# Gating guidance steps by their inputs' expected times, opening the last image with one chunk, and taking an image's last statistics from PSUM

## The chip, the cores and the metric

The kernel runs on one core of a Trainium2 chip. The metric is device time in microseconds, from the first to the last instruction of one execution. The kernel before takes 3024.74 us (median of 3 runs, 3021.86 to 3026.59); the profiled execution spans 3024.8 us. A difference of about 0.2% is the least that can be told from none.

## What is computed

The input x is (4, 256, 48, 48). Layer 0 adds to x an attention block: group norm, a 3x3 convolution with batch norm and ReLU, an 8-head attention over all 2304 pixels, a projection. Layer 1 adds to that a block of dynamic filters, and this is where the change lies:

```python
def _dyn_branch(x, w, d):                 # one dilation
    xp = jnp.pad(x, ((0, 0), (0, 0), (d, d), (d, d)))
    out, k = jnp.zeros_like(x), 0
    for dy in (-d, 0, d):
        for dx in (-d, 0, d):
            patch = xp[:, :, d + dy:d + dy + H, d + dx:d + dx + W]
            out = out + patch * w[:, k:k + 1]
            k += 1
    return out

guidance = _conv(x, W_cat, pad=1)         # 256 -> 45 channels, 3x3
outs = [x]
for i, d in enumerate((1, 6, 12, 24, 36)):
    w = jax.nn.softmax(guidance[:, 9 * i:9 * (i + 1)], axis=1)
    outs.append(_dyn_branch(x, w, d))
y = _conv(jnp.concatenate(outs, axis=1), W_scale, pad=0)   # 6*256 -> 256, 1x1
# then y is normalised over the whole batch: mean and variance of each channel
```

Here x is the group norm of the layer's input, and the layer's input is added to the result. So each pixel has 45 weights of its own, nine for each of five dilations, softmaxed over the nine.

## The kernel before

**Layout.** 256 channels are two halves (NH = 2) of 128 partitions. An image's 2304 pixels are six chunks (NCK = 6) of eight rows, CH = 384 pixels. The schedule is manual: each engine runs its instructions in the order in which the Python program emits them.

**Stages.** For each image: convolution and q, k, v (conv_qkv), attention, then dynamic_filters. The filters of image b are interleaved with conv_qkv of image b+1, a generator called `other`, of which every step is one matmul (or a small group) on PE and what follows from it. The filters of the last image (b = 3, `alone` in the code) have no other work beside them. Behind them comes finish, the batch norm over the whole batch and the output.

**Filters of one image.** A generator, weights(c), makes the softmaxed weights ("guidance") for two chunks c and c+1: 36 tap matmuls (18 for each chunk, which sit side by side in PE's columns, chunk c in PSUM partitions 0 to 44 and chunk c+1 in 64 to 108 of the tile pg; L1106), two copies to SBUF, one on ACT (L1116) and one on DVE (L1117), three transposes (tile pt, L1124), maximum, subtraction, exponential on ACT, sum, reciprocal and two products on DVE (L1137 to L1154), and for each of the two chunks three transposes back (tile pw, L1162), a rounding copy on ACT (L1169) and a subtraction of the rounded part on DVE (L1170), which gives the tile w. pg, pt and pw share one PSUM buffer (misc). In the profile a matmul of this kernel's 4-byte data shows as two records.

Then for each chunk, dilation and tap: PE spreads row k of w over all partitions by a matmul with pick (tile wb, L1299; three PSUM buffers, five when alone), DVE multiplies it with the shifted image (the first tap into cat, L1322; the others into prod, L1332, five buffers), and POOL adds prod to cat (L1349). When a cat is complete, PE mixes it with W_scale into py (L1240). In the last image some products skip POOL and are mixed straight from prod (`single`), where the program's clocks see POOL far behind PE. When a chunk is mixed, ACT copies py to SBUF (L1259), DVE takes the batch norm's statistics from the copy (L1263), and a DMA stores it.

**What sets the order.** The program keeps a model clock for each engine: clock(engine, ns, *after) starts an instruction behind the engine's last one and 150 ns behind each time in `after`. Before it emits a wb, it calls fill(until), where `until` is the expected time at which the wb buffer comes free. As long as PE's model clock is behind that time, fill emits, in this order of preference: a mix from `queue` whose input is expected by now, a guidance step if the pace allows one (pace[0] grows with the taps emitted, 27.6 steps in two chunks; pace[1] counts the steps taken), a step of `other`. Guidance of pair c+2 is paced over chunks c and c+1 and finished off, whatever is left, at the end of chunk c+1. The guidance of chunks 0 and 1 comes before the first tap ("opening"), with steps of `other` put in for as many ns as its negative yields say.

```python
def fill(until):
    while clock.t["PE"] < until:
        if queue and when(queue[0]) <= clock.t["PE"]:
            queue.pop(0)[-1]()
            continue
        if pace[1] < pace[0] and next(ahead, None) is not None:
            pace[1] += 1
            continue
        if next(other, None) is None:
            return
```

## Time and profile before

| stretch (us from the start) | what | length |
|---|---|---|
| 532 to 867, 1255 to 1594, 1981 to 2317 | filters of images 0, 1, 2 beside the next image's convolution | 335, 339, 336 |
| of these 571 to 853, 1294 to 1580, 2019 to 2303 | their taps | 282, 286, 284 |
| 2701 to 2737 | last image: projection, norm, opening | 36 |
| 2737 to 2981 | last image: taps | 244 |
| 2981 to 3017 | last mixes, batch norm, output | 36 |

The rest is the first convolution and four attentions, which the change doesn't touch. Over the span PE is busy 2834.9 us (94%), DVE 2419.1 (80%), ACT 1549.8 (51%) and POOL 1109.4 (37%). The granted clock of PE is 0.978 of full speed in the mean; in the filter stages it falls to one half for stretches of 3.4 to 10.2 us.

How to read a line of the timeline: start, time from the first start to the last end of the merged instructions, engine, source line, operation, output tile <- input tiles, shape, number of instructions; in brackets the idle time of the engine just before, and who released it. A line of the stage table has the stretch, its length and then busy us (and instructions) of PE, PEld, DVE, ACT and POOL, the clock granted to PE, the mean share of the DMA engines and GB/s. A busy share alone doesn't tell a bound: PE and POOL are both near 90% in the taps, so the places where one of them rests, and what the other does then, have to be laid side by side.

### The profile page before, as it was taken

To read this page: it belongs to the slowest core of one execution; us is meant where nothing else is said; L and a number is where in the kernel's file an instruction comes from. 1 tells how busy PE (TensorE), PEld (TensorE's weight loads), DVE (VectorE), ACT (ScalarE), POOL (GpSimd) and SP (SyncE) were. 2 spreads that over 40 slices of the span, in tenths; PEclk is the share of its full clock that TensorE was granted. 3 is DMA by queue.
4 is the path that set the end of the run, shared out by engine and by line. 5 is a ranking of instruction groups with operands and counts; after the bars stand their busy time and mean duration, and the time that the engine had idled before them with its cause. 6 is when DMAs were issued, how large, how long until landed. Compare 5 with 4: busy or idle time off the path is not lost. (4 is left out here: it accounts for less than half of the span.)

```text
span 3024.8 us, 42936 instructions
## 1 busy us (share of the span) xinstructions
PE 2834.9 (94%) x17454; PEld 1303.8 (43%) x17454; DVE 2419.1 (80%) x2312; ACT 1549.8 (51%) x1812; POOL 1109.4 (37%) x842
## 2 busy tenths in 40 slices
PE   7999999998999999989899999998899999989894
PEld 5622224465542222556662222346555222245552
DVE  6399999678869999767868999966776999976676
ACT  3489878201158888600228987830114888760003
POOL 1000000898930000389880000078894000007884
PEclk9999999999999999999999999999999999999997
DMA  4400000011030000001003000000002000012004
GB/s 173 97 1 6 7 11 7 27 37 32 22 79 6 3 4 12 22 25 36 29 11 79 6 6 12 6 27 27 21 6 42 3 5 6 12 66 112 1 1 178
DMA packets 77965, 95.52 MB, mean 32 GB/s; under 512 B 52144, under 2 KB 66752, under 8 KB 75968
## 3 DMA queue, kind: packets, MB, share of 16 engines
q1 hardware_dynamic: 76960, 87.31, 10.1%
q0 software_dynamic: 800, 5.41, 0.5%
q8 instruction: 138, 2.26, 0.3%
q14 instruction: 67, 0.55, 0.1%
HBM read 62.03 MB, written 30.67 MB: 31 GB/s over the span
## 5 line engine op out<-in xcount | busy, mean ns | idle before, releaser
L945 ACT ACTIVATE p<-se 128x1024 f32<-128x1024 f32 x1296 | 1259.0, 1026 | 243.0 <-PE se L936 217.2
L983 DVE TENSOR_TENSOR acc<-acc,p 128x2048 f32<-128x2048 f32 x536 | 1227.9, 2291 | 71.2 <-ACT p L945 24.3
L1349 POOL TENSOR_TENSOR cat<-cat,prod 128x752 f32<-128x752 f32 (+7 forms) x743 | 994.9, 1349 | 549.1 <-DVE prod L1332 507.5
L936 PE MATMUL se<-q,k 32*128 32x512 f32 (+1 forms) x5760 | 802.9, 591 | 6.0 <-DVE pad L1050 2.5
L1332 DVE TENSOR_TENSOR prod<-wb,pad 128x768 f32<-128x768 f32 (+7 forms) x768 | 553.5, 748 | 226.6 <-POOL cat L1349 151.0
L966 PE MATMUL num<-p,vT 128*32 128x512 f32 (+1 forms) x5760 | 692.9, 561 | 8.6 <-ACT scratch L988 7.4
L936 PEld LDWEIGHTS se<-q,k 32*128 32x128 f32 x5760 | 292.4, 183 | 519.7 <-issue 309.4
L738 POOL TENSOR_TENSOR cv_q<-pad,cv_q 128x600 f32<-128x600 f32 x3 | 4.1, 1353 | 1322.5 <-ACT cv_q L736 1322.5
L1299 PE MATMUL wb<-w,pick 128*128 128x384 f32 (+3 forms) x888 | 395.5, 495 | 11.7 <-DVE prod L1332 10.0
L1240 PE MATMUL py<-cat,wsc 128*128 128x384 f32 x960 | 354.9, 497 | 5.5 <-POOL cat L1349 5.3
L966 PEld LDWEIGHTS num<-p,vT 128*32 128x32 f32 x5760 | 121.7, 108 | 485.2 <-issue 437.5
L1299 PEld LDWEIGHTS wb<-w,pick 128*128 128x128 f32 x888 | 168.4, 194 | 151.9 <-DVE prod L1332 57.1
L1240 PEld LDWEIGHTS py<-cat,wsc 128*128 128x128 f32 x960 | 180.3, 193 | 92.4 <-POOL cat L1349 9.7
L844 PE MATMUL pc<-cv_q,u 128*128 128x288 f32 x576 | 170.2, 429 | 12.1 <-DVE cv_q L740 7.0
L844 PE MATMUL pc<-cv_k,u 128*128 128x288 f32 x576 | 161.1, 411 | 9.5 <-DVE yt L784 7.2
L1106 PE MATMUL pg<-pad,wcat 128*45 128x384 f32 x864 | 151.5, 494 | 1.5 <-DVE pad L590 1.5
L874 PE MATMUL pq<-hid,wqkv 128*128 128x384 f32 x384 | 136.1, 487 | 6.0 <-DVE yt L784 6.0
L844 PEld LDWEIGHTS pc<-cv_q,u 128*128 128x128 f32 x576 | 113.1, 201 | 41.9 <-DVE cv_q L740 7.0
L766 ACT ACTIVATE hid<-yt,bn_t_f,bn_s 128x288 f32<-128x288 f32 x64 | 39.4, 626 | 174.2 <-DVE yt L779 103.0
L844 PEld LDWEIGHTS pc<-cv_k,u 128*128 128x128 f32 x576 | 107.5, 191 | 38.6 <-DVE yt L784 8.4
L1322 DVE TENSOR_TENSOR cat<-wb,pad 128x768 f32<-128x768 f32 x120 | 113.9, 949 | 3.5 <-PE wb L1299 3.0
L983 DVE TENSOR_TENSOR acc<-p,p 128x2048 f32<-128x2048 f32 x36 | 82.5, 2292 | 40.3 <-ACT p L945 40.3
(209 smaller groups left out, 1613.5 us busy)
## 6 DMA issues: line engine op xcount, KB each, us to landing
pad<-in_x SPq DMA_DIRECT2D x14, 1152.0 KB, 14.9
u<-u_d SPq DMA_DIRECT2D x18, 768.0 KB, 4.3
x_d<-pad SPq DMA_DIRECT2D x48, 192.0 KB, 2.5
xst<-in_x SPq DMA_DIRECT2D x36, 192.0 KB, 2.4
y_d<-y SPq DMA_DIRECT2D x18, 384.0 KB, 2.8
u_d<-u SPq DMA_DIRECT2D x6, 768.0 KB, 3.7
y<-y_d SPq DMA_DIRECT2D x2, 2304.0 KB, 15.1
x<-x_d SPq DMA_DIRECT2D x2, 2304.0 KB, 22.3
```

What stands on the lines that cost most here:

```text
L844: nc.tensor.matmul(m, u[:, h, kx, o * P : (o + 1) * P], halves[g][:, h, i, :, kx : kx + WW], start=(h == 0 and kx == 0), stop=(h == NH - 1 ...
L874: nc.tensor.matmul(pq[:, :CH], wqkv[:, i, s, g * P : (g + 1) * P], hid[:, i, cols], start=(i == 0), stop=(i == NH - 1),)
L936: nc.tensor.matmul(ss[j // 2][:, j % 2, at : at + n], k_[r, g, m * P : (m + 1) * P], q[r, g, q0 : q0 + n], start=True, stop=True,)
L945: nc.scalar.activation(p[:, 2 * pair : 2 * pair + 2, :], ss[pair], AF.Exp, scale=QS)
L966: nc.tensor.matmul(st["num"][r, at : at + n], vT[:, m, g * P + j * D : g * P + (j + 1) * D], p[:, j, at : at + n], start=(m == 0 and not s ...
L983: nc.vector.tensor_tensor(st["acc"], other, p, ALU.add)
L1106: nc.tensor.matmul(pg[64 * s : 64 * s + NG, :CH], wcat[:, i, k, :], window(gn, i, (c + s) * R, k // 3 - 1, k % 3 - 1), start=(i == 0 and k ...
L1240: nc.tensor.matmul(to, wsc[:, n * NH + i, o * P : (o + 1) * P], rhs(i), start=(n == 0 and i == 0), stop=(last and i == NH - 1),)
L1299: nc.tensor.matmul(pw[:, : nr * WW], pick[:, k : k + 1].to_broadcast([P, P]), w[:, l0 * WW : l1 * WW], start=True, stop=True,)
L1322: nc.vector.tensor_tensor(catv, wb, src, ALU.mult)
L1332: nc.vector.tensor_tensor(pv, wb, src, ALU.mult)
L1349: nc.gpsimd.tensor_tensor(dst, dst, pv, ALU.add)
```

## The change

Four things, all in dynamic_filters.

1. **Expected times.** The steps of weights yield the model time at which the next step's input is expected (0.0 where it needs none) instead of a number of ns to fill. fill keeps that time in pace[2], and takes a guidance step only when PE's clock has reached it; such a step now stands ahead of the mixes. The purpose is that PE doesn't come to a transpose whose input isn't there.
2. **One chunk.** weights takes a tuple of chunks. For one chunk the two channel halves sit side by side in PE's columns where two chunks did: 18 matmuls, half sums in partitions 0 to 44 and 64 to 108, which a matmul with pick (a column sum of both) adds up while it transposes. The softmax then works on every second slot of e1.
3. **A plan.** Images 0 to 2 open with chunks (0, 1), as before. The last image opens with chunk 0 alone, makes chunk 1 during chunk 0, (2, 3) during chunk 1 and (4, 5) during chunks 2 and 3; the pace is set accordingly (`due`). What is left of a plan's steps is emitted when the next plan starts, or when a chunk needs its w.
4. **Statistics.** For the last chunk of an image bn_stats reads py in PSUM, not ACT's copy.

The diff, without its empty lines:

```diff
--- before.py
+++ after.py
@@ -1095,68 +1095,79 @@
                     spent[0] += got
                     ns -= got
-            def weights(c):
+            def weights(cs):
+                c, pair = cs[0], len(cs) == 2
                 pg = misc(f"pg_{b}_{c}")
-                for i in range(NH):
-                    for k in range(9):
+                for at in range(0, 9 * NH, 3 if pair else 6):
+                    for i, k in ((at // 9, at % 9 + d) for d in range(3)) if pair else (
+                        (0, at // 2 + d) for d in range(3)
+                    ):
                         for s in range(2):
+                            ii, cc = (i, c + s) if pair else (s, c)
                             nc.tensor.matmul(
                                 pg[64 * s : 64 * s + NG, :CH],
-                                wcat[:, i, k, :],
-                                window(gn, i, (c + s) * R, k // 3 - 1, k % 3 - 1),
+                                wcat[:, ii, k, :],
+                                window(gn, ii, cc * R, k // 3 - 1, k % 3 - 1),
                                 start=(i == 0 and k == 0),
-                                stop=(i == NH - 1 and k == 8),
+                                stop=((i == NH - 1 or not pair) and k == 8),
                             )
-                        if k % 3 == 2:
-                            clock("PE", 3 * MM)
-                            yield 3 * MM
+                    clock("PE", 3 * MM)
+                    if at + 3 < 9 * NH:
+                        yield 0.0
                 nc.scalar.copy(lg[:NG, :], pg[:NG, :CH])
                 nc.vector.tensor_copy(lg[64 : 64 + NG, :], pg[64 : 64 + NG, :CH])
-                clock("ACT", 480, clock.t["PE"])
-                clock("DVE", 560, clock.t["PE"])
-                yield -300.0
-                yield -300.0
+                yield 150 + max(
+                    clock("ACT", 480, clock.t["PE"]), clock("DVE", 560, clock.t["PE"])
+                )
                 pt = misc(f"pt1_{b}_{c}")
                 for t in range(TPC):
-                    nc.tensor.transpose(
-                        pt[:, t * P : (t + 1) * P], lg[:, t * P : (t + 1) * P], ident
-                    )
-                nb = 2 * TPC * len(DILATIONS)
+                    if pair:
+                        nc.tensor.transpose(
+                            pt[:, t * P : (t + 1) * P], lg[:, t * P : (t + 1) * P], ident
+                        )
+                    else:
+                        nc.tensor.matmul(
+                            pt[:, t * P : t * P + NG], lg[:, t * P : (t + 1) * P],
+                            pick.bitcast(F32), start=True, stop=True,
+                        )
                 lt = pt[:, : TPC * P].rearrange("p (t j) -> p t j", j=64)[:, :, :NG]
-                lt = lt.rearrange("p t (n k) -> p t n k", k=9)
-                ek, ek2 = (e1[:, :, j, :NG].rearrange("p t (n k) -> p t n k", k=9) for j in range(2))
+                step = 1 if pair else 2
+                lt = lt.rearrange("p t (n k) -> p t n k", k=9)[:, ::step]
+                ek, ek2 = (
+                    e1[:, ::step, j, :NG].rearrange("p t (n k) -> p t n k", k=9) for j in range(2)
+                )
+                shape = [P, 2 * TPC // step, len(DILATIONS)]
                 def each(t):
-                    return t.unsqueeze(3).to_broadcast([P, 2 * TPC, len(DILATIONS), 9])
-                yield 0
-                mx = small.tile([P, 2 * TPC, len(DILATIONS)], F32, tag="mx1", name=f"mx1_{b}_{c}")
+                    return t.unsqueeze(3).to_broadcast(shape + [9])
+                yield clock("PE", 550) + 150
+                mx = small.tile(shape, F32, tag="mx1", name=f"mx1_{b}_{c}")
                 nc.vector.tensor_reduce(mx, lt, AX.X, ALU.max)
-                clock("PE", 600)
                 clock("DVE", 430, clock.t["PE"])
-                yield -600.0
+                yield 0.0
                 nc.vector.tensor_tensor(ek, lt, each(mx), ALU.subtract)
-                clock("DVE", 430)
-                yield -600.0
+                yield clock("DVE", 430) + 150
                 nc.scalar.activation(ek, ek, AF.Exp)
-                yield -600.0
-                sm = small.tile([P, 2 * TPC, len(DILATIONS)], F32, tag="sm1", name=f"sm1_{b}_{c}")
+                yield clock("ACT", 430) + 150
+                sm = small.tile(shape, F32, tag="sm1", name=f"sm1_{b}_{c}")
                 nc.vector.tensor_reduce(sm, ek, AX.X, ALU.add)
                 clock("DVE", 430)
-                yield -600.0
+                yield 0.0
                 nc.vector.reciprocal(sm, sm)
                 clock("DVE", 330)
-                yield -600.0
+                yield 0.0
                 nc.vector.tensor_tensor(ek2, ek, each(sm), ALU.mult)
+                clock("DVE", 700)
+                yield 0.0
                 nc.vector.tensor_tensor(ek, ek, each(sm), ALU.mult)
-                clock("DVE", 1800)
-                for _ in range(3):
-                    yield 0
-                out = []
-                for s in range(2):
+                yield clock("DVE", 1100) + 150
+                for s in range(len(cs)):
                     pw = misc(f"pw_{b}_{c + s}")
                     for t in range(TPC):
                         nc.tensor.transpose(
@@ -1167,15 +1178,12 @@
                     w = work1.tile([P, CH], F32R, tag="w", name=f"w_{b}_{c + s}", bufs=4)
                     nc.scalar.copy(w, pw[:, :CH])
+                    yield clock("ACT", 480, clock("PE", 550))
                     nc.vector.tensor_tensor(
                         w[64:], pw[64:, :CH], w[64:].bitcast(F32), ALU.subtract
                     )
-                    out.append(w)
-                    clock("PE", 600)
-                    clock("ACT", 480, clock.t["PE"])
-                    clock("DVE", 560, clock.t["ACT"])
-                    yield -500.0
-                ready[c], ready[c + 1] = out
+                    ready[c + s] = w
+                    yield clock("DVE", 560, clock.t["ACT"]) + 150
             alone = b == B - 1
@@ -1196,9 +1204,10 @@
                     t = inside(gn, h, r0, r1 - r0)
                     normalize(t, t, norm.mean, norm.rstd, h)
             run(2000)
-            for got in weights(0):
-                if got < 0:
-                    run(-got)
+            clock.level()
+            for at in weights((0,) if alone else (0, 1)):
+                while clock.t["PE"] < at and next(other, None) is not None:
+                    pass
             queue = []
             ahead = iter(())
@@ -1209,11 +1218,13 @@
             def fill(until):
                 while clock.t["PE"] < until:
+                    if pace[1] < pace[0] and pace[2] <= clock.t["PE"]:
+                        at = next(ahead, None)
+                        if at is not None:
+                            pace[1:] = pace[1] + 1, at
+                            continue
                     if queue and when(queue[0]) <= clock.t["PE"]:
                         queue.pop(0)[-1]()
-                        continue
-                    if pace[1] < pace[0] and next(ahead, None) is not None:
-                        pace[1] += 1
                         continue
                     if next(other, None) is None:
                         return
@@ -1256,27 +1267,40 @@
                     yc = homes[c]
                 else:
                     yc = work1.tile([P, NH, CH], F32, tag="y", name=f"y_{b}_{c}")
-                nc.scalar.copy(yc, py.pop(c)[:, :, :CH])
+                of = py.pop(c)[:, :, :CH]
+                nc.scalar.copy(yc, of)
                 free["y"].append(clock("ACT", 800, clock.t["PE"]))
-                clock("DVE", 1100, free["y"][-1])
+                if c < NCK - 1:
+                    of = yc
+                    clock("DVE", 1100, free["y"][-1])
                 for o in range(NH):
-                    nc.vector.bn_stats(yst[:, o, b * NCK + c, :], yc[:, o, :])
+                    nc.vector.bn_stats(yst[:, o, b * NCK + c, :], of[:, o, :])
                 if not alone:
                     nc.sync.dma_start(out=y_d[b, :, :, cols], in_=yc)
             py = {}
-            pace = [0.0, 0]
+            pace = [0.0, 0, 0.0]
             STEPS = 24.0
+            plan = {0: (2, 3), 2: (4, 5)}
+            if alone:
+                plan = {0: (1,), 1: (2, 3), 2: (4, 5)}
             clock.level()
             free.update((tag, []) for tag in ("wb", "prod", "y"))
             for c in range(NCK):
                 if alone and c == 1:
                     back()
-                if alone and c == 2:
-                    flag_of(misc("pf")[:1, : B * NH])
-                if c % 2 == 0:
-                    ahead = weights(c + 2) if c + 2 < NCK else iter(())
-                    pace = [0.0, 0]
+                if c in plan:
+                    for _ in ahead:
+                        pass
+                    if alone and c == 2:
+                        flag_of(misc("pf")[:1, : B * NH])
+                    ahead = weights(plan[c])
+                    pace = [0.0, 0, 0.0]
+                    due = plan[c][0] - c
+                while c not in ready:
+                    next(ahead)
                 for o in range(NH):
                     queue.append(
                         (0.0, "", mix(c, 0, o, lambda i, c=c: window(gn, i, c * R, 0, 0)))
@@ -1349,7 +1373,7 @@
                         nc.gpsimd.tensor_tensor(dst, dst, pv, ALU.add)
                         summed = clock("POOL", added, end)
                         free["prod"].append(summed)
-                    pace[0] += STEPS * 1.15 * NH * nr * ncol * NCK / 2 / TAP_ELEMENTS
+                    pace[0] += STEPS * 1.15 * NH * nr * ncol * NCK / due / TAP_ELEMENTS
                     if j + 1 == len(taps) or taps[j + 1][0] != n:
                         for o in range(NH):
                             queue.append((
@@ -1359,9 +1383,6 @@
                                     n == len(DILATIONS) - 1,
                                 ),
                             ))
-                if c % 2 == 1:
-                    for _ in ahead:
-                        pass
             while queue:
                 fill(when(queue[0]))
                 if queue:
```

## Prediction

> **What bounds the kernel now.** I read the granted clock first (0.978), then the busy time by stage, because the page's shares mix four stages. The change touches only the filter stage of an image, which runs four times: 532 to 867, 1255 to 1594, 1981 to 2317, and alone from 2701. Busy time of the engines (PE, PEld, DVE, ACT, POOL, then granted clock, DMA share, GB/s) in the tap part of the first and of the last:
>
> ```profile
> 571.00:853.00 282.00, 258.97 (x1010) 165.43 (x1009) 216.90 (x328) 34.83 (x60) 254.37 (x188) 0.98 0.08 24
> ...
> 2737.00:2981.00 244.00, 222.10 (x857) 138.23 (x856) 174.98 (x253) 7.72 (x13) 216.83 (x164) 0.96 0.02 9
> ```
>
> PE is at 92% and 91%, POOL at 90% and 89%; ACT and DMA are no bound. Which of the two sets the pace is read from POOL's own timeline, where the bracket is idle time before a run of adds. In the last image:
>
> ```profile
> 2738.85 73.89 POOL L1349 TENSOR_TENSOR cat<-cat,prod 128x658 f32<-128x658 f32 x57 [432.16 <-DVE prod L1332]
> 2822.09 12.16 POOL L1349 TENSOR_TENSOR cat<-cat,prod 128x752 f32<-128x752 f32 x7 [9.34 <-DVE prod L1332]
> 2834.59 67.39 POOL L1349 TENSOR_TENSOR cat<-cat,prod 128x672 f32<-128x672 f32 x46 [0.34 <-DVE prod L1332]
> 2908.39 75.98 POOL L1349 TENSOR_TENSOR cat<-cat,prod 128x752 f32<-128x752 f32 x57 [6.41 <-DVE prod L1332]
> ```
>
> POOL never rests there except for 9.34 and 6.41 us. PE at the same moments:
>
> ```profile
> 2714.36 13.48 PE L1106 MATMUL pg<-pad,wcat 128*45 128x384 f32 x72 [1.45 <-DVE pad L590]
> ...
> 2811.07 0.55 PE L1124 MATMUL pt<-ident,lg 128*128 128x128 f32 x3 [1.22 <-DVE lg L1117]
> 2814.97 0.87 PE L1162 MATMUL pw<-ident,e 128*128 128x128 f32 x3 [3.36 <-DVE e L1154]
> 2817.01 0.90 PE L1162 MATMUL pw<-ident,e 128*128 128x128 f32 x3 [1.17 <-DVE w L1170]
> 2819.35 0.20 PE L1426 MATMUL pf<-okay,one 128*1 128x8 f32 x2 [1.44 <-DVE okay L1423]
> ```
>
> So the hole is guidance flushed in one piece at the end of an odd chunk: a serial chain PE, ACT, DVE, PE with no tap matmul (wb) between, so DVE and then POOL run dry. In the first image the same waits stand among other work:
>
> ```profile
> 596.48 0.55 PE L1124 MATMUL pt<-ident,lg 128*128 128x128 f32 x3 [3.31 <-DVE lg L1117]
> ...
> 624.98 0.90 PE L1162 MATMUL pw<-ident,e 128*128 128x128 f32 x3 [6.04 <-DVE e L1154]
> ...
> 690.85 0.90 PE L1124 MATMUL pt<-ident,lg 128*128 128x128 f32 x3 [3.54 <-DVE lg L1117]
> ```
>
> and POOL answers with a shorter hole:
>
> ```profile
> 573.01 55.31 POOL L1349 TENSOR_TENSOR cat<-cat,prod 128x658 f32<-128x658 f32 x39 [3.28 <-DVE prod L1332]
> 631.36 29.52 POOL L1349 TENSOR_TENSOR cat<-cat,prod 128x672 f32<-128x672 f32 x21 [3.03 <-DVE prod L1332]
> ```
>
> My reading: POOL sets the pace of the taps, PE close behind; a PE wait counts only as far as it opens a hole in POOL.
>
> [...] the DVE half of the second lg copy starts 5.93 us after the ACT half ended at 589.93, behind queued products, and PE's pt waits 3.31 us with ready work behind it. [...] mean clock 0.51 in 622 to 629, 0.57 in 690 to 694, 0.53 in 2813 to 2824, all just at these waits. [...] the product e<-e,sm takes 0.44 us with POOL idle and 1.05 to 1.87 us beside POOL. [...] the DVE lg copy [...] starts no earlier than 0.03 us after the ACT copy's end, in all six cases where DVE was free.
>
> **The change, part by part.**
>
> *Gating and priority in fill, images 0 to 2.* Steps are the same work; what changes is that pt, the sum, pw and the rest are emitted only when the clock model expects their inputs, and mixes or convolution steps take the place meanwhile. Old code had idle yields with no time attached, which fill used up at once when the pace had run ahead; that is the 6.04 us wait. The model's prices fit the trace (128x752 product 0.94 us, model 0.94; 128x672 add 1.49, model 1.49), so I expect most waits to go. Value, from POOL's holes just behind the guidance waits: image 0: 3.03; image 1: 0.49+0.53+0.30+1.16+3.88 = 6.4; image 2: 1.16+3.94 = 5.1; sum 14.5. The second pair of each image leads to holes of 1.10+2.84, 1.11+2.84+1.10 and 0.65+3.09+1.23 us, where DVE is also full with convolution outputs: I take a third of 13.9, 4.6. The following 2.4 us holes (image 0: 2.39+2.45+2.45) are DVE's convolution work alone, untouched. Against it I set 0.7 us of left-over wait per pair, six pairs, 4.2. Net: 14.9 us; bounds 0 and 14.5+13.9 = 28. The openings of these images stay: PE is already filled (its waits there are 0.18 and 0.19 us). Behind the last tap PE is busy for all 14 us with the last mixes and left-over convolution; unchanged.
>
> *Last image opens with one chunk.* 18 tap matmuls on two halves instead of 36. 72 records take 13.48 us here, 11.82 in image 0 at full clock, so the work is 11.8 and half of it 5.9; saved 5.9. One set of pw instead of two: the two DVE subtractions are 2734.34 and 2736.41, saved 2.07. Small operations on 135 instead of 270 columns: at 0.44 us for 270 and 0.16 for 2 columns, 135 cost 0.30; four of them on the chain, the exponential and the reciprocal save about 0.8. The matmul with pick in place of the transpose is three instructions again (0.55 us): nothing. Sum 8.8 us, all on the path, since nothing else runs.
>
> *Chunk 1 in chunk 0, pair 2/3 in chunk 1, pair 4/5 in chunks 2 and 3.* The flush at a chunk's end should find nothing left: a pace of 27.6 steps a chunk against some 14 (single) or 18 (pair), and guidance now comes before mixes, which took nearly every slot before. Removes 9.34+6.41 = 15.75 of POOL's holes. Added: 5.9 us of matmuls for chunk 1, 0.55 and 0.87 of transposes, about 7.4 us of PE that lay in the opening or were not there. PE and POOL share work through the "single" rule: one single less frees about 2.6 us of PE (8 records) and costs 1.5 of POOL, so 7.4 spread evenly costs 7.4 x 1.5/4.1 = 2.7. DVE gets 3 us more at 72% busy: hidden. The flag's matmul pf adds a wait: it now stands behind a full DVE queue, so PE may wait some 3 us, with five wb tiles of lead to cover it; I charge 2.3 for it and what remains of waits. Net 15.75-2.7-2.3 = 10.7; bounds 3 and 15.75.
>
> *Statistics from PSUM.* The copy is 0.80 us (2987.41 to 2988.21) and bn_stats starts at 2988.24. If both read at once, 0.8 is gained; [...] I take 0.
>
> Sum: 14.9+8.8+10.7 = 34.4; 3024.7-34.4 = 2990.
>
> **Rivals.** *Waits move rather than go* (20%): [...] the ACT step is not tied to the DVE step before it, so a step is still emitted early. Then images 0 to 2 give nothing, the last one gives its opening and a third of 15.75: 14, giving 3011. For it: e at 1.87 us. Against: the model already reserves 0.7 and 1.1 for these products. *PE sets the pace* (13%): every PE wait and half-clock stretch counts, 6.85+7.03 plus (6.8+3.4)/2, about 19 an image. POOL's total holes without the first limit that to 15.0, 18.7 and 17.1; with two thirds of these, 34, and 22 in the last image, 2969. Against: POOL's gapless runs. *Slower* (7%): fill finds too little slack alone, so chunk 1 is flushed before its turn (9.3 more of hole), the old two flushes stay, PE has 2.7 more, and postponed mixes hold the four cat buffers, 4 us in each of the other images: -8.8+9.3+2.7+12 = +15, giving 3040. Against: between 2737 and 2778 PE serves a mix or guidance step after nearly every pair of wb, so there are slots enough.
>
> **How the numbers follow.** Main case 60%, 2975 to 3005 by its bounds. The range 2970 to 3012 takes in the first rival and the edge of the second; below it lies some of the second, above it the slower case. Faster by over 0.2% (under 3018.7): 0.60+0.13+0.17 = 0.90; same 0.04; slower 0.06.
>
> **What would show it.** In the last image the first POOL add near 2730 rather than 2738.85, POOL holes of 9.34 and 6.41 gone, more adds on POOL; pg matmuls spread between wb; pt and pw waits under 1.5 us; clock near 1.0 in the tap parts; POOL's end about 19 us earlier. In images 0 to 2 the tap part near 277 instead of 282 to 286. bn_stats still right behind the copy. Wrong if pt or pw waits of over 3 us reappear, if POOL has a new hole before chunk 1, or if PE, with no wait left, runs solid while POOL idles.

## The result, and the profile after

The changed kernel takes 3003.16 us (median of 4 runs, 3001.14 to 3007.46), the kernel before 3023.3 us beside it: a ratio of 0.9934, 95% interval 0.9917 to 0.9952, so 20 us (15 to 25) faster. Measured once more in the next section it was 0.992 (0.9907 to 0.9934). The forecast was 2990 us, with 2970 to 3012 as its range: the direction holds and the time lies in the range, but of 34 us forecast 20 came.

The last image first. A hole below is idle time of POOL between two runs of adds. POOL's own timeline after (start, length, then idle time before in brackets):

```profile
2725.83 79.65 POOL L1373 TENSOR_TENSOR cat<-cat,prod 128x658 f32<-128x658 f32 x60 [424.71 <-DVE prod L1356]
2806.26 3.54 POOL L1373 TENSOR_TENSOR cat<-cat,prod 128x752 f32<-128x752 f32 x2 [0.77 <-DVE prod L1356]
2810.01 155.26 POOL L1373 TENSOR_TENSOR cat<-cat,prod 128x752 f32<-128x752 f32 x110 [0.21 <-DVE prod L1356]
```

The holes of 9.34 and 6.41 us are gone; what is left is 0.77 us at the flag's matmul. But POOL now works 155 us in one piece, and does 172 adds (60, 2 and 110) where it did 167. PE in the same image, the opening, then the guidance of chunks 2 and 3 and the flag's matmul pf:

```profile
2708.25 8.49 PE L1111 MATMUL pg<-pad,wcat 128*45 128x384 f32 x36 [1.45 <-DVE pad L590]
2717.90 0.87 PE L1134 MATMUL pt<-pick,lg 128*128 128x45 f32 x6 [1.16 <-DVE lg L1122]
2721.22 0.88 PE L1173 MATMUL pw<-ident,e 128*128 128x128 f32 x3 [2.45 <-DVE e L1168]
...
2778.20 0.49 PE L1129 MATMUL pt<-ident,lg 128*128 128x128 f32 x3
2794.71 0.49 PE L1173 MATMUL pw<-ident,e 128*128 128x128 f32 x3
2800.49 0.55 PE L1173 MATMUL pw<-ident,e 128*128 128x128 f32 x3 [0.43 <-DVE w L1182]
2803.77 0.20 PE L1447 MATMUL pf<-okay,one 128*1 128x8 f32 x2 [2.73 <-DVE okay L1444]
```

No guidance step in the taps waits over half a microsecond. Now image 0, PE's guidance matmuls and then POOL:

```profile
592.98 0.49 PE L1129 MATMUL pt<-ident,lg 128*128 128x128 f32 x3
617.12 0.55 PE L1173 MATMUL pw<-ident,e 128*128 128x128 f32 x3 [0.25 <-DVE e L1168]
...
679.93 0.49 PE L1129 MATMUL pt<-ident,lg 128*128 128x128 f32 x3
```

```profile
576.12 41.40 POOL L1373 TENSOR_TENSOR cat<-cat,prod 128x658 f32<-128x658 f32 x31 [4.62 <-DVE prod L1356]
617.99 93.37 POOL L1373 TENSOR_TENSOR cat<-cat,prod 128x752 f32<-128x752 f32 x63 [0.47 <-DVE prod L1356]
714.11 1.13 POOL L1373 TENSOR_TENSOR cat<-cat,prod 128x192 f32<-128x192 f32 x2 [2.75 <-DVE prod L1356]
719.81 3.63 POOL L1373 TENSOR_TENSOR cat<-cat,prod 128x752 f32<-128x752 f32 x2 [4.57 <-DVE prod L1356]
726.10 5.20 POOL L1373 TENSOR_TENSOR cat<-cat,prod 128x752 f32<-128x752 f32 x3 [2.66 <-DVE prod L1356]
733.84 6.73 POOL L1373 TENSOR_TENSOR cat<-cat,prod 128x752 f32<-128x752 f32 x4 [2.54 <-DVE prod L1356]
```

The waits of 3.31, 6.04 and 3.54 us are gone and so is the 3.03 us hole they made. Yet POOL's holes in image 0 add up to 17.6 us, where they were 18.3: the first is 4.62 and no longer 3.28, and those beside the convolution's outputs at 710 to 735 make 12.5 (12.0 before). Image 0 gains least. Without the first hole, which belongs to the opening, the holes of images 0, 1 and 2 went from 15.0, 18.7 and 17.1 us to 13.0, 11.9 and 11.8.

So I cut each execution by DVE's instructions: *opening* from the attention's last acc add to the first tap product, *taps* to the last tap product, *tail* to the next attention's first acc add (last image: to the end), *attention* from first to last acc add. Means over images 0 to 2, over the three attentions behind a filter stage, and the last image, in us:

| kernel | opening | taps | tail | attention | last opening | last taps | last tail |
|---|---|---|---|---|---|---|---|
| before | 38.0 | 284.0 | 19.6 | 381.3 | 35.7 | 243.6 | 44.2 |
| after | 40.3 | 280.5 | 15.2 | 383.8 | 30.1 | 237.5 | 44.2 |
| after, once more | 40.3 | 280.7 | 15.2 | 383.0 | 31.0 | 237.2 | 44.1 |

Per image 0 to 2: +2.3-3.4-4.4 = -5.5, so 16.5 for three. Attentions: +2.5 each, so 7.4 lost again, in code that the change does not touch. Last image: -5.6-6.1 = -11.7. With 1.8 us more ahead of the first filter stage, -16.5+7.4-11.7+1.8 = -19.0; the two spans (3024.8 and 3005.7) differ by 19.1. The tail and the attention were not in my forecast at all; this is the end of image 0 after, PE and then ACT:

```profile
855.32 2.85 PE L1251 MATMUL py<-cat,wsc 128*128 128x384 f32 x8 [0.45 <-POOL cat L1373]
859.50 2.85 PE L1251 MATMUL py<-cat,wsc 128*128 128x384 f32 x8 [1.33 <-POOL cat L1373]
864.43 2.22 PE L936 MATMUL se<-q,k 32*128 32x512 f32 x12 [2.09 <-DVE yst L1277]
867.67 2.08 PE L936 MATMUL se<-q,k 32*128 32x512 f32 x4 [1.01 <-ACT p L945]
```

```profile
862.42 0.80 ACT L1271 COPY y<-py 128x768 f32<-128x768 f32 x1 [7.22 <-PE py L1251]
866.59 2.85 ACT L945 ACTIVATE p<-se 128x1024 f32<-128x1024 f32 x3 [3.37 <-DMA y_d<-y]
```

Before, the end of image 0 on PE and its first exponential were:

```profile
857.25 2.74 PE L1240 MATMUL py<-cat,wsc 128*128 128x384 f32 x8
859.83 7.07 PE L895 MATMUL pv<-wqkv,hid 128*128 128x256 f32 x32
...
868.87 3.77 ACT L945 ACTIVATE p<-se 128x1024 f32<-128x1024 f32 x4 [1.35 <-PE se L936]
```

Before, 7 us of the next image's v matmuls stood behind the last mix. After, none do: all 72 pv records lie among the taps, where before 40 stood ahead of the last mix and 32 behind it. In their place stand three new waits: PE's scores wait 2.09 us for the statistics, which now hold the PSUM buffer of py; ACT's first exponential waits 3.37 us for the store of the last y, on whose memory p lies; and PE, which has rested 0.45, 1.33 and 2.09 us, runs the first 7 to 10 us of the attention almost wholly at half clock. Three stretches behind the filter stages (the mean granted clock is the third number from the right, 0.51, 0.51 and 0.52):

```profile
866.00:873.00 7.00, 5.99 (x22) 1.22 (x20) 2.10 (x1) 3.88 (x4) 0.00 (x0) 0.51 1.01 195
1586.00:1596.00 10.00, 9.91 (x40) 2.05 (x32) 2.29 (x1) 5.18 (x6) 0.00 (x0) 0.51 1.03 201
2306.00:2316.00 10.00, 9.88 (x40) 2.58 (x40) 2.29 (x1) 4.72 (x5) 0.00 (x0) 0.52 1.01 205
```

### The profile page after: what moved, and what is told of

Read it like the earlier page. It is cut to its first block, busy times and chain, and to the rows that moved or that the text cites. A ratio compares the mean times of both kernels' runs of the same rounds, so it can differ in the third digit from the quotient of the medians.

```text
span 3005.7 us, 42904 instructions
## 1 busy us (share of the span) xinstructions
PE 2842.5 (95%) x17423; PEld 1283.2 (43%) x17423; DVE 2427.0 (81%) x2319; ACT 1551.0 (52%) x1814; POOL 1121.7 (37%) x847
## 5 line engine op out<-in xcount | busy, mean ns | idle before, releaser
L1373 POOL TENSOR_TENSOR cat<-cat,prod 128x752 f32<-128x752 f32 (+7 forms) x748 | 1007.1, 1357 | 519.9 <-DVE prod L1356 477.6
L936 PE MATMUL se<-q,k 32*128 32x512 f32 (+1 forms) x5760 | 812.4, 597 | 9.6 <-DVE yst L1277 6.3
L844 PE MATMUL pc<-cv_q,u 128*128 128x288 f32 x576 | 160.1, 411 | 10.4 <-DVE cv_q L740 6.4
L1121 ACT COPY lg<-pg 45x384 f32<-45x384 f32 x13 | 6.1, 473 | 247.7 <-PE pg L1111 247.7
L1346 DVE TENSOR_TENSOR cat<-wb,pad 128x768 f32<-128x768 f32 x120 | 113.8, 948 | 11.7 <-PE wb L1323 11.4
## 6 DMA issues: line engine op xcount, KB each, us to landing
pad<-in_x SPq DMA_DIRECT2D x14, 1152.0 KB, 14.8
```

The source lines that it names most:

```text
L844: nc.tensor.matmul(m, u[:, h, kx, o * P : (o + 1) * P], halves[g][:, h, i, :, kx : kx + WW], start=(h == 0 and kx == 0), stop=(h == NH - 1 ...
L936: nc.tensor.matmul(ss[j // 2][:, j % 2, at : at + n], k_[r, g, m * P : (m + 1) * P], q[r, g, q0 : q0 + n], start=True, stop=True,)
L1346: nc.vector.tensor_tensor(catv, wb, src, ALU.mult)
L1373: nc.gpsimd.tensor_tensor(dst, dst, pv, ALU.add)
```

## The experiments

Where the runs are compared with each other, "the changed kernel" is its repeat at 3002.5 us; ratios are to the kernel before, measured beside each. The kernel before itself had medians of 3025.8 to 3027.1 us beside them, so a few microseconds between two kernels (0.2% are 6 us) are not told from none by the times alone; there the stages of the profiles have to speak. The condition that a guidance step waits for its expected time (pace[2]) is called the gate, and guidance emitted in one piece, because no earlier place was found for it, is called flushed.

### The changed kernel once more

> The changed kernel again, as the reference of this group of runs. 3003 us, 20 us under the kernel before. If the first attention, in which both programs are the same up to then, takes 382.5 us here as in the profile of before and not 384.9, its 2.4 us were chance; the later attentions should still start at half clock for 6.8 to 10.2 us, since PE rests 0.45+1.33+2.09 us before each of them.

3002.5 us, ratio 0.992 (0.9907 to 0.9934). The first attention took 382.5 us this time, so its 2.4 us were chance; the three later ones took 384.5, 384.4 and 380.2 against 382.7, 382.4 and 378.9 before, each with a half-clock stretch of 6.8 us at its start. So 5.1 us of the loss in the attentions came again. It hangs on whether the half clock comes, and that is not fixed: see the last section.

### The last image opens with a pair

```diff
-            for at in weights((0,) if alone else (0, 1)):
+            for at in weights((0, 1)):
-            if alone:
-                plan = {0: (1,), 1: (2, 3), 2: (4, 5)}
```

> The changed kernel with the last image opened by the pair (0, 1) and the plan of the other images; gating and statistics stay. Theory A (the gate alone removes the flushes, and POOL's 9 extra adds are paid for chunk 1's guidance among the taps): the opening takes 35.7 us again (5.6 more), the adds go back from 303 towards 294 and the taps from 237.5 to some 232, so the whole is 0 to 3 us slower than the changed kernel, about 3004. Theory B (the plan with one chunk is the gain of the last image): the 11.7 us are lost, 3015.

3010.91 us, ratio 0.9942 (0.9928 to 0.9956), 8.4 over the changed kernel. The opening takes 37.5 us instead of 31.0, the taps 238.6 instead of 237.2, and POOL still does 172 adds. (The expectations counted POOL's semaphore instructions with the adds: their 294 and 303 are 167 and 172.) So both theories were half right: the taps keep their gain without the one-chunk plan, and that plan is worth 6.5 us in the opening. The extra adds do not come from chunk 1's guidance, since they are there with the pair too.

### Statistics from the copy

```diff
-                if c < NCK - 1:
+                if True:
                     of = yc
```

> The changed kernel with the statistics of an image's last chunk taken from ACT's copy again. Theory A (in images 0 to 2 the first exponential waits for the store of the last y, which ends after the statistics): PE starts the scores 1.1 us earlier in three images, but the first exponential stays where it is; 0 to 1 us faster, 3002 to 3003; in the last image no change, since with either source the statistics start behind the copy. Theory B (statistics from PSUM hold the buffer, and this wait brings the half clock at the start of three attentions): 1.1+2.4 us in each of three images, 10 us faster, 2993.

2999.32 us, ratio 0.9908 (0.9893 to 0.9924): 3.2 faster, between the theories, and the intervals overlap. The profile shows both mechanisms. The tail is only 0.4 us shorter, for the exponential still waits for the store:

```profile
860.11 0.80 ACT L1271 COPY y<-py 128x768 f32<-128x768 f32 x1 [7.22 <-PE py L1251]
864.31 3.77 ACT L945 ACTIVATE p<-se 128x1024 f32<-128x1024 f32 x4 [3.40 <-DMA y_d<-y]
```

But PE starts the scores right behind the copy, two of the three attentions stay at full clock in their first 7 to 10 us (mean clock 1.00, 0.83 and 1.00), and their mean length is 381.7 us instead of 383.0. The last image's tail is 44.2 us with the copy and 44.1 with PSUM: part four of the change gains nothing in the last image. That it costs something at the other three borders is read from the wait of 2.09 us; the 3.2 us between the medians are too little to show it.

### The order and the expected times in fill

Both undone, then each alone:

```diff
 # both: mixes first, and guidance as soon as the pace allows
+                    if queue and when(queue[0]) <= clock.t["PE"]: ...
-                    if pace[1] < pace[0] and pace[2] <= clock.t["PE"]: ...
-                    if queue and when(queue[0]) <= clock.t["PE"]: ...
+                    if pace[1] < pace[0]: ...
 # mixes first alone: the two blocks exchanged, the condition on pace[2] kept
 # ungated alone: the order kept, the condition on pace[2] dropped
```

> The changed kernel with the old order in fill: mixes first, then guidance, and guidance without looking at the expected time. Plan, opening and statistics stay. Theory A (the expected times and the order are the gain of images 0 to 2 and remove the flush of the last): waits of 3 to 6 us before pt and pw come back, images 0 to 2 lose 9 us, and the last image, where guidance is again flushed before chunks 1, 2 and 4, loses 15: 3025 or more. Theory B (the plan is the gain): 3 us slower at most, 3006.

> The changed kernel with only the order in fill undone: mixes before guidance, while guidance still waits for its expected time. Theory A1 (in the last image it is the order that removes the flush, since a mix is nearly always ready and takes the slot): the last image flushes as in the kernel with both undone, 329 us instead of 312; images 0 to 2 as in the changed kernel, 336 each; the whole 3018. Theory A2 (the expected times do it): like the changed kernel, 3003.

> The changed kernel with only the expected times undone in fill: guidance first, as soon as the pace allows. Theory A1 (order): the last image stays near 313 us with waits of some us before pt and pw in its taps, images 0 to 2 within 1 us of 336, the whole 3003 to 3007. Theory A2 (expected times): waits of 3 to 6 us per step, POOL holes of 5 us and more, last image 325 or more, 3016.

| kernel | us | ratio (interval) | opening | taps | tail | last taps | adds there |
|---|---|---|---|---|---|---|---|
| the changed kernel | 3002.5 | 0.992 (0.9907 to 0.9934) | 40.3 | 280.7 | 15.2 | 237.2 | 172 |
| both undone | 3018.22 | 0.997 (0.9959 to 0.9982) | 40.2 | 282.2 | 14.2 | 254.4 | 167 |
| mixes first | 3017.88 | 0.9972 (0.9962 to 0.9983) | 39.3 | 280.2 | 15.2 | 253.8 | 167 |
| ungated | 3022.27 | 0.9991 (0.9983 to 0.9999) | 39.3 | 283.2 | 15.0 | 252.8 | 173 |

Neither half does anything for the last image's taps by itself; without either they are longer than before the change (243.6 us), since the new plan brings chunk 1's guidance in among them. The last column shows where the extra adds come from: they are there whenever guidance stands ahead of the mixes, with the gate or without. With mixes first, guidance is flushed as before, now also before chunk 1. POOL:

```profile
2761.09 10.60 POOL L1373 TENSOR_TENSOR cat<-cat,prod 128x752 f32<-128x752 f32 x6 [5.74 <-DVE prod L1356]
...
2815.93 12.34 POOL L1373 TENSOR_TENSOR cat<-cat,prod 128x752 f32<-128x752 f32 x7 [13.68 <-DVE prod L1356]
...
2900.92 76.05 POOL L1373 TENSOR_TENSOR cat<-cat,prod 128x752 f32<-128x752 f32 x57 [6.11 <-DVE prod L1356]
```

With guidance first and ungated, PE stands in the middle of the chunks:

```profile
2744.22 0.88 PE L1173 MATMUL pw<-ident,e 128*128 128x128 f32 x3 [5.35 <-DVE e L1168]
2785.33 0.55 PE L1129 MATMUL pt<-ident,lg 128*128 128x128 f32 x3 [2.33 <-DVE lg L1122]
2792.36 0.87 PE L1173 MATMUL pw<-ident,e 128*128 128x128 f32 x3 [6.48 <-DVE e L1168]
```

In images 0 to 2, though, both of them undone cost only 0.4 us per image (opening, taps and tail together 336.6 against 336.2): the taps are 1.5 us longer and the tails 1.0 shorter. A wait of 3.96 us before a pw does come back in image 0, as theory A has it, but little of it reaches the end of the stage. All 72 pv records lie among the taps in all three of these kernels. So most of the gain there comes neither from the gate nor from the order.

### The last y where no p lies

With the statistics from the copy as above, and

```diff
                 if alone:
                     yc = homes[c]
+                elif c == NCK - 1:
+                    yc = e1.rearrange("p t a j -> p (t a j)").rearrange("p (h c) -> p h c", h=NH)
```

> The changed kernel with the statistics from ACT's copy, and in images 0 to 2 that copy of the last chunk put into e1, which is idle by then, and not into a y buffer, where the next attention's p lies. Theory A (the store of that y is what the first exponential waits for): the first exponential comes 5 us behind POOL's last add and not 7.2; 2 us less in each of three images than with the statistics alone undone (2999), so 2993. Theory B (PE's scores or the half clock set the start of the attention): 2999 as there.

2987.47 us, ratio 0.9878 (0.9863 to 0.9893): 11.9 under the run with the statistics alone undone. ACT at the end of image 0:

```profile
859.71 0.80 ACT L1273 COPY e<-py 128x768 f32<-128x768 f32 x1 [7.20 <-PE py L1251]
861.86 3.77 ACT L945 ACTIVATE p<-se 128x1024 f32<-128x1024 f32 x4 [1.35 <-PE se L936]
```

The exponential comes 2.15 us behind the copy's start instead of 4.2, and waits for PE alone. So the store on p's memory is shown to be what the exponential waited for. The tails are 12.7 us instead of 14.8 (6.1 for three, as theory A has it), and all three attentions start at full clock and take 381.1 us, as before the change. The two profiles are 10.8 us apart; most of what remains lies in the taps (280.3 instead of 281.3 us each) and in the attentions (0.6 each). Why the taps became shorter was not tested.

### More products mixed singly

```diff
-BEHIND = 4000.0
+BEHIND = 1000.0
```

> The changed kernel with BEHIND = 1000 instead of 4000, so that in the last image 23 products and not 20 skip POOL and are mixed singly. Theory A (POOL alone sets the pace of the last image's taps, its adds having grown from 294 to 303, while PE rests 16 us): 3 adds less are 4.5 us less, taps 233, the whole 2998. Theory B (both are even, PE's rests being waits for cat and prod that more mixing only moves): within 1 us, 3002.

2998.97 us, ratio 0.9906 (0.989 to 0.9921), 3.5 faster with overlapping intervals. In the profile POOL does 169 adds instead of 172 and is busy 225.8 instead of 230.8 us, and the last taps take 235.0 instead of 237.2. Three products less were 5 us of POOL, of which 2.2 reached the end; holes of 4.2 us in all opened in POOL. So POOL alone doesn't set the pace there, against theory A.

### Both together

> The two edits that helped, together: statistics from ACT's copy, the last y of images 0 to 2 in e1, and BEHIND = 1000. If they are independent (one at the ends of images 0 to 2, one in the last image's taps), 2987.5-3.5 = 2984. If they are not, 2987.

2984.44 us, ratio 0.9863 (0.9848 to 0.9878), the fastest kernel here: 42 us under the kernel before, 18 under the change. That the two gains add up is not shown: it is 3.0 us under the kernel with the y apart alone, their intervals overlap, and in their profiles the last taps take 236.4 and 237.4 us.

### The v matmuls held back

```diff
             for t in range(0, NT, 2):
+                while t == 6 and hold[0]:
+                    yield None
...
+            hold[0] = False
             run(1e9)
```

> The changed kernel with the last six groups of the next image's v matmuls (48 records, 10.4 us by the program's clocks) held back in images 0 to 2 until the last mix is out, which is where they lay in the kernel before. All else as in the changed kernel. Theory A (the gain of images 0 to 2 is that these matmuls no longer stand behind the last mix; DVE and POOL set the taps): the tails are 19.6 us again and not 15.2, the attentions start at full clock, 2 us less each, taps as they were or 2 us shorter: 4.4-2 = 2 to 3 us more per image, 3007 to 3011. Theory B (the gain is the removed guidance waits, and PE's work counts wherever it lies): 3002 to 3004, and image totals near 336.

3018.64 us, ratio 0.9976 (0.9966 to 0.9986), 16 slower than the changed kernel. The tails are 22.8 us instead of 15.2, the taps 280.6 instead of 280.7, the attentions 381.1 instead of 383.0. PE at the end of image 0:

```profile
855.35 2.85 PE L1255 MATMUL py<-cat,wsc 128*128 128x384 f32 x8 [1.33 <-POOL cat L1377]
858.03 10.52 PE L897 MATMUL pv<-wqkv,hid 128*128 128x256 f32 x48
```

Two things follow. Ten microseconds of PE work taken out of the end of the taps do not shorten them, so PE's load doesn't set their pace there. And the same work behind the last mix counts: 7.7 of its 10.5 us. The images take 343.2 us each, against 336.2 in the changed kernel and 341.5 before. But the run holds back more than the expectation says: before, 32 records (7.07 us) stood behind the last mix, not 48, and the other 3.45 us went in ahead of it. With these taken off, my estimate is 339.8 us, so some 3.6 us of the gain per image come from this left-over, which went in among the taps, and the rest from elsewhere.

### A lighter convolution output

```diff
-                    result(1, d34, -2.0, d12)
-                    result(2, s34, -4.0, s12)
+                    if b:
+                        for r, y in ((1, d12), (2, s12)):
+                            relu(g, o, r, y)
+                            clock("ACT", 630, clock("DVE", 1200))
+                    else:
+                        result(1, d34, -2.0, d12)
+                        result(2, s34, -4.0, s12)
```

> The changed kernel, which in images 1 to 3's convolution leaves out two of the five DVE operations of the output step of product 0 (rows 1 and 2 of every four then lack one term), eight operations of some 1.2 us beside POOL in each of the stages of images 0 to 2. The model clocks are charged as before, so the order on the engines is the same. Theory A (the four holes of 2.5 to 4.6 us in POOL at these outputs, 12.5 us in the stage, are DVE's queue and hold up the taps): holes go down to some 4 us, taps from 281 to 273, 3 x 8 us faster: 2979. Theory B (PE sets the pace of the stage): taps by less than 2 us shorter, 2998 or more.

2989.2 us, ratio 0.9873 (0.9858 to 0.9888): 13.3 faster, and 12.2 us less in the taps of the three images. POOL in image 0:

```profile
711.59 1.14 POOL L1378 TENSOR_TENSOR cat<-cat,prod 128x192 f32<-128x192 f32 x2 [0.73 <-DVE prod L1361]
716.83 3.64 POOL L1378 TENSOR_TENSOR cat<-cat,prod 128x752 f32<-128x752 f32 x2 [4.10 <-DVE prod L1361]
722.26 5.20 POOL L1378 TENSOR_TENSOR cat<-cat,prod 128x752 f32<-128x752 f32 x3 [1.80 <-DVE prod L1361]
729.14 11.79 POOL L1378 TENSOR_TENSOR cat<-cat,prod 128x752 f32<-128x752 f32 x7 [1.68 <-DVE prod L1361]
```

The four holes fall from 12.5 to 8.3 us and the taps from 280.7 to 276.6: by as much. So a hole in POOL at these outputs is a loss of the stage, microsecond for microsecond. It is half of what I expected. Three of the four are DVE's queue: they fall from 7.95 to 4.21 us, and the other three operations stay. The largest (4.57 us after the change, 4.10 here) is not: ahead of it DVE itself rests and waits for PE's next wb. DVE, after the change and here:

```profile
717.93 0.96 DVE L1346 TENSOR_TENSOR cat<-wb,pad 128x768 f32<-128x768 f32 x1 [3.63 <-PE wb L1323]
...
714.94 0.96 DVE L1351 TENSOR_TENSOR cat<-wb,pad 128x768 f32<-128x768 f32 x1 [3.17 <-PE wb L1328]
```

In both kernels PE works through eight records of a mix and four of the convolution just before that wb, so this hole comes from PE's order.

### One chunk for all images

As the fastest kernel, and `plan = {0: (1,), 1: (2, 3), 2: (4, 5)}` with weights((0,)) for images 0 to 2 as well.

> As e6_apart_behind, and images 0 to 2 open with one chunk and the plan of the last image. Theory A (POOL and DVE set the pace behind the opening): openings 6.5 us shorter, taps as they were, 5 us less in each: 2969. Theory B (PE's work sets the total of the stage: the guidance matmuls that leave the opening push convolution out behind the last mix, 16.8 us of it by the program's clocks): openings and taps shorter, tails 8 to 12 us longer, nothing gained or 3 us lost per image: 2984 to 2995.

3010.22 us, ratio 0.9947 (0.9934 to 0.9961), 26 slower than the fastest. Openings 33.0 us instead of 39.3, taps 277.6 instead of 280.3, but tails 29.3 instead of 12.7. Behind the last mix now lie all 72 pv and 4 pq records, and 4 more pq behind the last tap. The stage has nearly the same work on PE as in the fastest kernel and takes 7.5 us longer per image: it is a matter of where the work ends up. What doesn't go in among the taps counts behind them. Theory B had the direction right and the cost too low.

## Why the prediction was right or wrong

The time lies inside the range partly by luck. The three parts that the sum of 34.4 us was made of gave 21.9: 10.2 in the taps of images 0 to 2, 5.6 in the last opening, 6.1 in the last taps. What was not forecast nearly cancelled: the tails gained 13.2 us, the openings lost 6.9 and the attentions 7.4.

**Last image opens with one chunk: right, too high.** Predicted 8.8 us, measured 5.6 (6.5 against the kernel that differs in this alone). Of the missing 3.2 us, 1.5 are not the opening's own: the last matmuls of the projection, which the change doesn't touch, ran at a lower clock this time (1.00 in the mean over these matmuls before, 0.63 after).

```profile
2705.28 2.82 PE L1041 MATMUL pp<-ao,wp 128*128 128x384 f32 x8 [2.73 <-DVE ao L1009]
...
2697.86 4.34 PE L1041 MATMUL pp<-ao,wp 128*128 128x384 f32 x8 [2.74 <-DVE ao L1009]
```

The first line is before, the second after; in the run with the statistics from the copy they took 2.82 us, and the opening 28.2. Of the rest, 0.9 is that the 36 records took 8.49 us, not 13.48 less 5.9; 0.75 that with one w the first wb stands on the path, so that the second w was worth 1.3 and not 2.07; and 0.3 that pt is a plain matmul now, six records and 0.87 us where I counted three and 0.55. Some 0.2 us came back in the norm ahead of it.

**Chunk 1 in chunk 0, flushes gone: mechanism right, one term mis-sized.** POOL's two holes of 15.75 us became 0.8 to 1.0, as forecast. But I had POOL take over 1.8 products' adds (2.7 us). It took five: 20 single products instead of 25, POOL busy 222.0 before and 231.0 after, 9.1 us. So 15 us of holes less 9 us of adds are the 6.1 that the taps gained, against 10.7 forecast. The extra adds come with the order, guidance ahead of the mixes, and not with the gate or with chunk 1's guidance (table above, and 172 in the kernel that opens with a pair). This fits the rule for single products, which compares POOL's clock with PE's clock and the waiting mixes: the order delays mixes. The rule itself was not taken apart. The flag's wait was 2.73 us on PE and 0.77 on POOL, inside the 2.3 charged.

**Gating in images 0 to 2, 14.9 us: the holes right, their cause in the main not.** The holes behind guidance waits did go, from 14.7 to 1.4 us in the three images, as forecast. The holes beside the convolution outputs, of which I had counted 4.6 us as guidance's, stayed: 36.1 us before, 35.2 after, and in image 0 after they are made by DVE's queue and, the largest, by PE's order. POOL's adds took 1.2 us longer per image (busy 260.2 before, 261.4 after), for which I had no term. That leaves the 10.2 us measured. But with the gate and the order both undone the holes behind guidance waits are 8.2 us and not 14.7, and the taps 1.5 us longer per image, 4.5 of 10.2. So under half of the taps' gain is the gate's and the order's, and without them the three tails are 2.9 us shorter together. What brought the rest was not isolated: with both undone the kernel still differs from the one before in the steps of weights, their prices on the model clocks and the place of the left-over steps.

**Openings "stay" and tails "unchanged": wrong.** The openings became 2.3 us longer (1.3 in several kernels with the same opening). Ten records of convolution stand between the last pw and the first wb, where four did, because the last wait for w is now filled. The tails became 4.4 us shorter, because 32 records of v no longer stand behind the last mix. "PE is busy for all 14 us" was read from the profile correctly; that this work could move, and that it was on the path there, I did not ask. Why more of the convolution is emitted among the taps was not isolated; it is so without gate and order too.

**Attention: not in the sum, and the change's cost.** The tail that was freed uncovered two waits it had hidden: the store of y before the first exponential, and the statistics before the scores. The half clock, for 6.83 to 10.24 us, came behind them. The attentions lost 7.4 us in the first profile, 5.1 in the second. I had priced the statistics at nothing, which is right for the last image (as on lg before, DVE starts on py 0.03 us after the end of ACT's copy of it, and the tail stays at 44.2 us), but I did not ask who waits for the buffer that they now hold.

**The rivals.** "PE sets the pace" is wrong for the end of the taps (held-back matmuls) and right for one hole in each image, 4.57 us in image 0, beside the convolution outputs; beyond that, PE's work counts where it doesn't fit among the taps (one chunk for all). "Waits move rather than go" did not come as it was put: the waits before pt and pw went. But others appeared at the attention's door. One reading for this rival was too narrow: beside POOL the product e<-e,sm took 0.44 to 1.87 us in the trace before, not 1.05 to 1.87. The forecast of 2990 was too low by 13 us: 14.9 for images 0 to 2 against a net 9.1 (16.5-7.4), and 19.5 for the last image against 11.7.

## What to carry to other kernels

When work leaves the end of a stage, look at what it was hiding: here a store on memory that the next stage reuses and a PSUM buffer with a late reader, waits of 2.09 and 3.37 us at the end of image 0 and, in 20 of 24 places, a half clock on top, undone by taking the statistics from the copy and putting one tile elsewhere. A hole in the engine that sets the pace is worth its length only if the engine ahead of it has nothing else to be late with; take the hole apart by what fills that engine's queue before counting it (of 12.5 us in image 0, 7.95 were DVE's queue and 4.57 PE's order). And a step that waits for an input needs both to be placed late enough and to be preferred once it is ready: in the last image either alone lost all of the gain in the taps (253.8 and 252.8 us, against 243.6 before and 237.2 with both).

## What the runs showed of the hardware

Before the attentions behind a filter stage PE rested 0.45, 1.33 and 2.09 us in the changed kernel, with 2.85 us of work between the rests, and then ran at half clock for 6.83 us (image 0) or 10.24 us (images 1 and 2). But the half clock did not always follow such rests. Over eight profiles, with a rest of 2.09 us before the scores in all 24 places, the half clock came in 20 and stayed away in four, as at the end of image 0 in the lighter convolution:

```profile
859.60 1.99 PE L941 MATMUL se<-q,k 32*128 32x512 f32 x12 [2.09 <-DVE yst L1282]
...
859.60:866.60 7.00, 5.77 (x40) 1.68 (x40) 1.00 (x1) 4.32 (x5) 0.00 (x0) 1.00 1.04 222
```

With 0.89 or 0.93 us in place of 2.09 the scores started at full clock in nine places of nine. In the filter stages before, and at the attentions after, half-clock stretches last 3.41, 6.83 or 10.24 us, which are one, two and three times the same length. What decides between them was not tested.

In the changed kernel three transposing matmuls against pick took 0.76 us at full clock (six records, chunk 1 of the last image), three transposes against ident 0.49 us (three records, image 0), although the output of the first is narrower, 45 columns against 128.
